# A graph layer's set-up: destination places in 128 rows, and the order of transfers on SP

## The chip, the cores and the metric

The kernel runs on one core of a Trainium2 chip. The metric is the time on the device in microseconds (us), as a median of runs. A core has engines with instruction queues of their own: PE (TensorE, matmuls), DVE (VectorE), ACT (ScalarE), POOL (GpSimd) and SP (SyncE). Each takes its queue in order. SP and ACT issue plain DMA transfers; POOL issues indirect ones (gathers by a list of row numbers). All share 16 DMA engines. An instruction can wait on semaphores that other engines or landed transfers raise, and what stands behind it in the same queue waits too.

## The reference

One message-passing layer of a graph network with 12,500 nodes, 412,500 edges (sorted by destination) and 96 channels:

```python
def _mlp(h, W, b, gamma, beta):
    h = relu(h @ W + b)
    mu, var = mean(h, axis=0), mean(square(h - mu), axis=0)
    return gamma * (h - mu) * rsqrt(var + EPS) + beta

node_feat = _mlp(x, W_node, ...)
edge_feat = _mlp(edge_attr, W_edge, ...)
message = concat([x[src], x[dst], edge_feat], axis=1)
message = _mlp(message, W_msg, ...)
agg = segment_sum(message, dst, 12500)
out = layernorm(x + agg + node_feat)
```

All normalisations are over the rows (all nodes or all edges), so statistics over every edge must be known before the edge features can be used in a message.

## The kernel before

Edges go in groups of 512 (four tiles of 128), four groups to a block: 806 groups, 202 blocks. The message's first product is split over the three parts of its input: a first table `p_tab` = x·W (source part) and a second table `q_tab` (destination part) are computed once per node and kept in DRAM. For each group, `p_tab`'s rows are gathered by source (L290, four indirect DMAs per group, on POOL). Destinations are sorted, so a group's edges fall into a window of 31 nodes; the window's rows of `q_tab` are loaded as they are, and an edge's place in its window picks its row through a matmul.

The places are needed in two forms. In one (`rel`) edges lie on partitions. In the other, `rel_d` in DRAM, they lie in a row, edge after edge, so that the main loop can load them beside the edges' attributes (L355). `rel_d` is computed by the loop at L194 to L201: the destinations `dlin` are loaded in two-group pieces of a layout with 101 rows of eight groups each (RW = 8·512), the groups' first nodes are loaded (`first`), DVE subtracts (L200), and ACT's queue stores (L201). The loads are on SP (L196, L198).

Before the main loop comes a set-up: 1. `table` for `p_tab`; 2. weights, `rel` and a check (`flag`); 3. the places; 4. `table` for `q_tab`, seven chunks of 14 column groups, each ending in a store on SP (L152); 5. `nodes`: matmuls of all nodes (L210), statistics (L212), normalisation (L218, L219), and 13 pieces `y0` = centred x + node feature, copied by DVE (L228) and stored on SP (L231); 6. `edge_norm`: the edge features' statistics, 202 steps in 26 chunks of eight. A chunk's attributes are loaded by SP (L246, two buffers), and a step is three matmuls (L250), one ACTIVATE (L253) and three BATCH_NORM_STATS2 (L255).

During all this POOL already gathers for the first 104 groups. They go, in 26 blocks of 16 gathers, into a tile `stage` with two buffers, and SP stores each block to DRAM (`spill`, L304); the main loop reads it back. After the 26 blocks POOL gathers 30 more groups into the ring that the main loop uses. Block k's gathers can start once store k-2 has landed.

The order of the instructions on SP and POOL is written out by hand in `fast` (the block under `manual_schedule`); the other engines' order comes from a scheduler. `blocks` is a generator: `next(store)` puts one block's gathers on POOL and its store on SP at that place in the program. As SP is in order, a store stands behind everything that SP issues before it, whatever that waits for.

The order is: places; second table with stores of blocks 0 and 1 behind its fourth and seventh chunk; stores 2 and 3; nodes with store 4 behind the sixth y0 and store 5 behind the thirteenth; edge statistics with one store ahead of the loads of chunks 2, 3, 4, 6, 7, 8, 9, 11 and so on (four of five); the last store; the ring.

The main loop works through all groups, per group four matmuls (L380), an addition of the gathered rows (L386), a relu (L387) and four matmuls that sum messages by place and collect the second moments (L395). The end normalises and adds y0.

Of the kernel before, what the change touches and what calls it, by code (L numbers as in the profile page):

```python
# [11 lines left out]
F32 = mybir.dt.float32  # L12
I32 = mybir.dt.int32
AF = mybir.ActivationFunctionType
OP = mybir.AluOpType
# [5 lines left out]
N, C, E, ED = 12500, 96, 412500, 4  # L21
EPS = 1e-5
P = 128
# [3 lines left out]
GT, GE, BG = 4, 512, 4  # L27
# [3 lines left out]
NTP, NGP = NBL * BG * GT, NBL * BG  # L31
EP = NGP * GE
EK = ED + 1
Q = 32
NS = 3
RW = 8 * GE

# [11 lines left out]
WN = 31  # L51
# [20 lines left out]
def gnn(ctx, tc, t):  # L72
    nc = tc.nc
    const = ctx.enter_context(tc.tile_pool(name="const", bufs=1))
    dram = ctx.enter_context(tc.tile_pool(name="dram", bufs=1, space=DRAM))
# [1 line left out]
    q_tab = dram.tile([NN, C], F32, name="q_tab")  # L77
    y0_d = dram.tile([-(-NB // NBY), P, NBY * C], F32, name="y0_d")
    spill = dram.tile([SPILL // BG, P, BG, GT * C], F32, name="spill")
    rel_d = dram.tile([1, EP], F32, name="rel_d")  # L80


    w_msg = const.tile([C, 3, C], F32, name="w_msg")
# [32 lines left out]
    base = const.tile([1, NGP], I32, name="base")  # L116
# [9 lines left out]
    def norm(aggr, gamma, beta, name):  # L126

        s = const.tile([C, 3], F32, name=f"norm_{name}")
        nc.scalar.activation(s[:, 2:3], aggr[:, 1:2], AF.Sqrt, bias=eps[:C], scale=1.0)  # L129
        nc.vector.reciprocal(s[:, 2:3], s[:, 2:3])  # L130
        nc.vector.tensor_mul(s[:, 0:1], s[:, 2:3], gamma)  # L131
        nc.vector.tensor_mul(s[:, 2:3], s[:, 0:1], aggr[:, 0:1])  # L132
        nc.vector.tensor_sub(s[:, 1:2], beta, s[:, 2:3])  # L133
        return s[:, 0:1], s[:, 1:2]


    def table(out, w, work, ps, queues):

        rows = out.rearrange("(p b) f -> p b f", b=NB)
        for c in range(0, NB, CH):  # L140
            r = work.tile([P, CH, C], F32, name="trow", bufs=3)
            for j, i in enumerate(range(0, CH, NBK)):
                n = min(NBK, CH - i)
                pt = ps.tile([P, NBK, C], F32, name="pt", bufs=4)
                for g in range(n):
                    k = COL[c + i + g]
                    nc.tensor.matmul(pt[:, g, :], xp[:, k:k + P], w, start=True, stop=True)  # L147
                if j % 2:
                    nc.scalar.activation(r[:, i:i + n, :], pt[:, :n, :], AF.Copy)  # L149
                else:  # L150
                    nc.vector.tensor_copy(r[:, i:i + n, :], pt[:, :n, :])
            queues[c // CH % len(queues)].dma_start(rows[:, c:c + CH, :], r)  # L152
            yield
# [9 lines left out]
    for i in range(NS):  # L163
        k, n = Q * i, C - Q * i
# [24 lines left out]
        nc.vector.tensor_reduce(most, po, axis=AX.X, op=OP.max)  # L189
        nc.vector.tensor_scalar(flag, most, 0.0, None, op0=OP.is_gt)  # L190

    with tc.tile_pool(name="lin", bufs=2) as work:
        shape = "o (p g e) -> (o p) g e"
        for i in range(0, RW // GE, 2):  # L194
            lin = work.tile([EP // RW, 2, GE], I32, name="lin")
            nc.sync.dma_start(lin, t["dlin"].rearrange(shape, g=RW // GE, e=GE)[:, i:i + 2, :])  # L196
            first = work.tile([EP // RW, 2], I32, name="first")
            nc.sync.dma_start(first, t["base"].rearrange("o (p g) -> (o p) g", g=RW // GE)[:, i:i + 2])  # L198
            rlin = work.tile([EP // RW, 2, GE], F32, name="rlin")
            nc.vector.tensor_tensor(rlin, lin, first.unsqueeze(2).to_broadcast([EP // RW, 2, GE]), op=OP.subtract)  # L200
            nc.scalar.dma_start(rel_d.rearrange(shape, g=RW // GE, e=GE)[:, i:i + 2, :], rlin)  # L201

    def nodes():

# [30 lines left out]
    def edge_norm():  # L235

        with tc.tile_pool(name="es", bufs=2) as work, tc.tile_pool(name="es1", bufs=1) as one, \
                tc.tile_pool(name="es_ps", bufs=2, space=PSUM) as ps:
            stats = one.tile([P, NS, NBL, 6], F32, name="estats")
            for b in range(NBL):  # L240
                if b % J == 0:
                    yield
                    ea = work.tile([P, J, GE], F32, name="ea")
                    n = min(J, NBL - b)
                    for i in range(NS):
                        nc.sync.dma_start(ea[Q * i:Q * i + 2 * EK, :n, :],  # L246
                                          t["ea"][EK * i:EK * (i + 2), b:b + n, :])
                pr = ps.tile([P, NS, GE], F32, name="pr")
                for i in range(NS):
                    nc.tensor.matmul(pr[:, i, :], wide[Q * i:Q * i + 2 * EK, :],  # L250
                                     ea[Q * i:Q * i + 2 * EK, b % J, :], start=True, stop=True)
                r = work.tile([P, NS, GE], F32, name="r")
                nc.scalar.activation(r, pr, AF.Relu)  # L253
                for i in range(NS):
                    nc.vector.bn_stats(stats[:, i, b, :], r[:, i, :])  # L255

            part = one.tile([P, NS, 2], F32, name="part")
            square = one.tile([P, NS], F32, name="square")
            for i in range(NS):
                nc.vector.bn_aggr(part[:, i, :], stats[:, i, :, :].rearrange("p a b -> p (a b)"))  # L260
            nc.vector.tensor_mul(square, part[:, :, 0], part[:, :, 0])
            nc.vector.tensor_add(part[:, :, 1], part[:, :, 1], square)
            pick = one.tile([P, NS, C], F32, name="pick")
            nc.vector.memset(pick, 0.0)
            for i in range(NS):
                for o in range(-P * i % C - C, P, C):
                    lo, hi = max(o, 0), min(o + C, P)
                    if lo < hi:
                        to = pick[:, i, lo - o:hi - o]
                        nc.vector.tensor_add(to, to, ident[:, lo:hi])  # L270
            pm = ps.tile([C, 2], F32, name="pr")
            for i in range(NS):
                nc.tensor.matmul(pm, pick[:, i, :], part[:, i, :], start=i == 0, stop=i == NS - 1)
            aggr = one.tile([C, 2], F32, name="eaggr")
            nc.vector.tensor_scalar(aggr, pm, float(NBL * GE) / E, None, op0=OP.mult)
            sq = one.tile([C, 1], F32, name="sq")
            nc.vector.tensor_mul(sq, aggr[:, 0:1], aggr[:, 0:1])
            nc.vector.tensor_sub(sq, aggr[:, 1:2], sq)
            nc.vector.tensor_scalar(aggr[:, 1:2], sq, 0.0, None, op0=OP.max)
            a_e, c_e = norm(aggr, v["g_edge"], v["beta_edge"], "edge")  # L280
            pb = ps.tile([1, C], F32, name="pr")
            nc.tensor.matmul(pb, c_e, w_msg[:, 2, :], start=True, stop=True)
            nc.vector.tensor_add(bias, pb, b_msg)
            nc.vector.tensor_scalar(w_e, w_msg[:, 2, :], a_e, None, op0=OP.mult)

    def fast(ring):
# [8 lines left out]
        def ahead_of(g):  # L295
            return gather(g, ring.tile([P, GT, C], F32, name="pg"))

        def blocks():

            for b in range(SPILL // BG):  # L300
                pg = ring.tile([P, BG, GT, C], F32, name="stage", bufs=2)
                for i in range(BG):
                    gather(b * BG + i, pg[:, i, :, :])
                nc.sync.dma_start(spill[b], pg.rearrange("p g a c -> p g (a c)"))  # L304
                yield


        store = blocks()
        with tc.manual_schedule(engines={ET.SP, ET.Pool}):
            with tc.tile_pool(name="tab_w", bufs=1) as work, tc.tile_pool(name="tab_ps", bufs=2, space=PSUM) as ps:  # L310
                for i, _ in enumerate(table(q_tab, w_msg[:, 1, :], work, ps, (nc.sync,))):
                    if i in (3, 6):
                        next(store)
            next(store)
            next(store)
            for i, _ in enumerate(nodes()):
                if i in (5, 12):
                    next(store)
            xpool.close()
            for i, _ in enumerate(edge_norm()):  # L320
                if i > 1 and i % 5:
                    next(store, None)
            for _ in store:
                pass
            got = {g: ahead_of(g) for g in range(SPILL, SPILL + RING)}

        with tc.tile_pool(name="fix", bufs=1) as fix, tc.tile_pool(name="msg", bufs=2) as work, \
# [92 lines left out]
            last, n, ahead = None, 0, SPILL + RING  # L420
# [20 lines left out]
            d = fix.tile([C, C], F32, name="d")  # L441
# [9 lines left out]
    def general():  # L451

        with tc.tile_pool(name="gd", bufs=1, space=DRAM) as gd, tc.tile_pool(name="gfix", bufs=1) as fix, \
# [136 lines left out]
            for b in range(NB):  # L590
# [7 lines left out]
                nc.vector.tensor_copy(agg[:, b * P:(b + 1) * P], px)  # L598

    fast(ring)  # L600
    rpool.close()
    bad = nc.values_load(flag, min_val=0, max_val=1, skip_runtime_bounds_check_because="a comparison's result")
# [4 lines left out]
    with tc.tile_pool(name="fin", bufs=2) as work, tc.tile_pool(name="fin_ps", bufs=2, space=PSUM) as ps:  # L607
# [6 lines left out]
        d = const.tile([C + 1, C], F32, name="dm")  # L614
# [3 lines left out]
        for i in range(0, NB, NBY):  # L618
            n = min(NBY, NB - i)
# [55 lines left out]
```

## Time and profile before

| | us |
|---|---|
| median of 11 runs | 5677.29 (5660.83 to 5681.44) |
| the profiled execution, its own time | 5676.63 |
| its span in the profile | 5674.9 |
| first gather / last of the 26 blocks' gathers | 54.6 / 1010.8 |
| first gather of the ring / of the main loop | 1012.1 / 1250.5 |
| busy: PE, DVE, ACT, POOL | 3489.2, 1838.8, 1128.7, 3067.8 |
| mean granted TensorE clock | 0.659 |

In the profile, a line of a group gives source line, engine, operation, tiles out<-in and count, then busy time and mean ns of one, then the idle time of the engine just before and what ended most of it. A line of the timeline gives start, duration, engine ("q" for its queue, where DMAs are issued), source line, operation, tiles and count, and in brackets the idle time before it and what ended it. "remote" there is an event whose sender the profile could not match. A line of the table by stretches gives the stretch, its length, the busy time of each engine, the granted clock of TensorE, the share of the DMA engines and the rate.

### The profile page before, as it was taken

The numbers are of one execution on the slowest core, as the hardware profiler recorded it, in microseconds if no ns is written. First come the engines' busy times: TensorE is split into PE (matmuls) and PEld (weight loads), VectorE is DVE, ScalarE is ACT, GpSimd is POOL, SyncE is SP. The second block draws the span as 40 slices with busy tenths as digits, with TensorE's granted clock in tenths as the row PEclk, the third lists the DMA queues.
The fourth block names the chain that finished last, engine by engine and source line by source line (L and its number), as shares of the span: only waits on it lengthen the run. The fifth ranks groups of instructions, "written<-read, shape, count | busy, mean of one in ns | idle before, by whom it ended". The sixth has DMA issues, their size and how long they took to land. (4 is left out here: it accounts for less than half of the span.)

```text
span 5674.9 us, 52840 instructions
## 1 busy us (share of the span) xinstructions
PE 3489.2 (61%) x16561; PEld 2604.3 (46%) x16561; DVE 1838.8 (32%) x4227; ACT 1128.7 (20%) x1304; POOL 3067.8 (54%) x3231
## 2 busy tenths in 40 slices
PE   3445565236766666676666666666666666666668
PEld 3331111015554555555445554545555455554547
DVE  1134555143232232322222322323233232322326
ACT  0123444121111111111111111111111111111113
POOL 2244444725655655555565556655655655556650
PEclk9955555556666666666676766666666676666767
DMA  3132232211111111111111111111111111111112
GB/s 118 73 95 59 63 67 65 52 36 40 42 41 42 37 42 41 40 42 40 37 41 41 42 41 37 42 40 42 42 41 41 38 42 40 41 41 36 42 34 73
DMA packets 154490, 271.03 MB, mean 48 GB/s; under 512 B 83723, under 2 KB 84107, under 8 KB 153198
## 3 DMA queue, kind: packets, MB, share of 16 engines
q0 software_dynamic: 103136, 158.62, 11.6%
q1 hardware_dynamic: 47572, 96.59, 6.0%
q10 hardware_dynamic: 3496, 12.36, 0.7%
q8 instruction: 136, 2.23, 0.2%
q14 instruction: 150, 1.23, 0.1%
HBM read 225.97 MB, written 41.37 MB: 47 GB/s over the span
## 5 line engine op out<-in xcount | busy, mean ns | idle before, releaser
L290 POOL DMA_INDIRECT pg<-p_tab,src x2807 | 2667.7, 950 | 1847.9 <-issue 759.3
L380 PE MATMUL z<-rhs,left 128*128 128x96 f32 x6446 | 1316.1, 348 | 644.6 <-issue 337.9
L380 PEld LDWEIGHTS z<-rhs,left 128*128 128x128 f32 x6446 | 1169.6, 260 | 1088.5 <-issue 596.7
L395 PE MATMUL pa<-h 128*97 128x128 f32 x6446 | 1240.1, 355 | 690.4 <-ACT h L387 495.3
L395 PEld LDWEIGHTS pa<-h 128*97 128x97 f32 x6446 | 1080.1, 228 | 750.1 <-ACT h L387 539.4
L387 ACT ACTIVATE h<-hs 128x384 f32<-128x384 f32 x806 | 419.8, 521 | 2980.8 <-DVE hs L386 1381.3
L398 DVE TENSOR_TENSOR agg<-pa,agg 97x31 f32 x806 | 151.2, 188 | 1948.6 <-remote 836.5
L290 POOL DMA_INDIRECT stage<-p_tab,src x416 | 399.1, 959 | 611.0 <-DMA spill<-stage 432.6
L386 DVE TENSOR_TENSOR hs<-z,pg 128x384 f32<-128x384 f32 x702 | 390.3, 556 | 999.1 <-remote 512.3
L250 PE MATMUL pr<-ea,wide 10*128 10x512 f32 x1212 | 406.6, 1108 | 412.4 <-ACT r L253 292.7
L371 PE MATMUL pr<-ea,we 6*127 6x512 f32 x1404 | 517.3, 813 | 157.7 <-issue 83.9
L255 DVE BATCH_NORM_STATS2 estats<-r 128x6 f32<-128x512 f32 x606 | 372.1, 681 | 445.8 <-ACT r L253 315.5
L373 ACT ACTIVATE left<-pr 96x2048 f32<-96x2048 f32 x202 | 376.5, 1864 | 621.7 <-remote 309.6
L374 DVE TENSOR_SCALAR left<-pr 31x2048 f32<-31x2048 f32 x202 | 462.9, 2292 | 45.1 <-ACT left L373 40.1
L250 PEld LDWEIGHTS pr<-ea,wide 10*128 10x128 f32 x1212 | 113.9, 307 | 703.7 <-ACT r L253 516.3
L253 ACT ACTIVATE r<-pr 128x1536 f32<-128x1536 f32 x202 | 292.7, 1451 | 589.9 <-remote 401.0
L371 PEld LDWEIGHTS pr<-ea,we 6*127 6x127 f32 x1404 | 131.6, 230 | 218.8 <-issue 128.1
L382 DVE TENSOR_TENSOR h<-rel,iota 128x124 f32<-128x124 f32 x806 | 208.1, 279 | 2.0 <-issue 0.4
L399 DVE TENSOR_TENSOR gram<-pa,gram 97x97 f32<-97x97 f32 x806 | 202.1, 251 | 12.9 <-DVE agg L398 6.5
L147 PE MATMUL pt<-w_msg,xp 96*128 96x96 f32 x392 | 85.5, 423 | 138.3 <-ACT trow L149 130.6
L147 PEld LDWEIGHTS pt<-w_msg,xp 96*128 96x128 f32 x392 | 84.1, 332 | 139.5 <-ACT trow L149 131.5
L371 PE MATMUL pr<-eae,we 6*127 6x512 f32 x208 | 75.9, 796 | 7.2 <-issue 7.0
(97 smaller groups left out, 507.2 us busy)
## 6 DMA issues: line engine op xcount, KB each, us to landing
pg<-p_tab,src POOLq DMA_INDIRECT x2807
spill<-stage SPq DMA_DIRECT2D x26, 768.0 KB
pb<-spill SPq DMA_DIRECT2D x26, 768.0 KB
rhs<-q_tab SPq DMA_DIRECT2D x806, 11.6 KB
ea<-in_ea SPq DMA_DIRECT2D x75, 160.0 KB
ea<-in_ea SPq DMA_DIRECT2D x352, 20.0 KB
stage<-p_tab,src POOLq DMA_INDIRECT x416
q_tab<-trow SPq DMA_DIRECT2D x7, 672.0 KB
```

The lines of the kernel that those rows point to most:

```text
L250: nc.tensor.matmul(pr[:, i, :], wide[Q * i:Q * i + 2 * EK, :], ea[Q * i:Q * i + 2 * EK, b % J, :], start=True, stop=True)
L253: nc.scalar.activation(r, pr, AF.Relu)
L255: nc.vector.bn_stats(stats[:, i, b, :], r[:, i, :])
L290: nc.gpsimd.indirect_dma_start(out=pg[:, i, :], out_offset=None, in_=p_tab[:, :], in_offset=bass.IndirectOffsetOnAxis(ap=src[:, k:k + 1], ...
L371: nc.tensor.matmul(pr[:, i, :], we[Q * i:Q * i + EK + 1, :], ea[Q * i:Q * i + EK + 1, :], start=True, stop=True)
L373: nc.scalar.activation(x[:C, :n, :], pr[:C, :n, :], AF.Relu)
L374: nc.vector.tensor_scalar(x[C:C + WN, :n, :], pr[C:, :n, :], 0.0, None, op0=OP.is_equal)
L380: nc.tensor.matmul(z[:, i, :], left[s % 2][:KR, g % BG, i * P:(i + 1) * P], rhs[:KR, s % 2, g % BG, :], start=True, stop=True)
L382: nc.vector.tensor_tensor(h[:, :, C + 1:C + 1 + WN], rel[:, g, :].unsqueeze(2).to_broadcast([P, GT, WN]), iota[:, None, :].to_broadcast([P ...
L386: nc.vector.tensor_add(hs[:, :n, :], z[:, :n, :], pg[:, :n, :])
L387: nc.scalar.activation(h[:, :n, :C], hs[:, :n, :], AF.Relu)
L395: nc.tensor.matmul(pa[:, :C + 1 + WN], h[:r, i, :C + 1], h[:r, i, :C + 1 + WN], start=i == 0, stop=i == n - 1)
```

## The change

1. The places are computed in 128 rows of seven groups (RW = 7; the destinations are padded on the host from 808 to 896 groups). `first` comes as an input of its own in that layout and is loaded once. Pieces have two groups each, the last one.
2. They stand in a function `places`, called after the second table and store 2. A piece's store is issued one piece later, on SP instead of ACT.
3. The stores of the blocks move: stores 0, 1, 2 behind the table's second, fifth and seventh chunk; store 3 behind the places; 4 and 5 behind the third and ninth y0; store 6 ahead of the loads of statistics chunk 0, and from then about 73 in a hundred chunks (three of four) have one ahead of them.

The number of gathers, stores and statistics steps is the same, and the main loop and the end are untouched.

```diff
-RW = 8 * GE
+RW = 7
...
-    rel_d = dram.tile([1, EP], F32, name="rel_d")
+    rel_d = dram.tile([1, P * RW * GE], F32, name="rel_d")
...
-    with tc.tile_pool(name="lin", bufs=2) as work:
-        shape = "o (p g e) -> (o p) g e"
-        for i in range(0, RW // GE, 2):
-            lin = work.tile([EP // RW, 2, GE], I32, name="lin")
-            nc.sync.dma_start(lin, t["dlin"].rearrange(shape, g=RW // GE, e=GE)[:, i:i + 2, :])
-            first = work.tile([EP // RW, 2], I32, name="first")
-            nc.sync.dma_start(first, t["base"].rearrange("o (p g) -> (o p) g", g=RW // GE)[:, i:i + 2])
-            rlin = work.tile([EP // RW, 2, GE], F32, name="rlin")
-            nc.vector.tensor_tensor(rlin, lin, first.unsqueeze(2).to_broadcast([EP // RW, 2, GE]), op=OP.subtract)
-            nc.scalar.dma_start(rel_d.rearrange(shape, g=RW // GE, e=GE)[:, i:i + 2, :], rlin)
+    def places():
+
+        with tc.tile_pool(name="lin", bufs=2) as work, tc.tile_pool(name="lin1", bufs=1) as one:
+            first = one.tile([P, RW], I32, name="first")
+            nc.sync.dma_start(first, t["first"])
+            rows = rel_d.rearrange("o (p g e) -> (o p) g e", g=RW, e=GE)
+            parts = [slice(i, min(i + 2, RW)) for i in range(0, RW, 2)]
+            lins = []
+            for i in range(len(parts) + 1):
+                if i < len(parts):
+                    n = parts[i].stop - parts[i].start
+                    lins.append(work.tile([P, n, GE], I32, name="lin"))
+                    nc.sync.dma_start(lins[i], t["dlin"][:, parts[i], :])
+                    rlin = work.tile([P, n, GE], F32, name="rlin")
+                    nc.vector.tensor_tensor(rlin, lins[i], first[:, parts[i]].unsqueeze(2).to_broadcast([P, n, GE]),
+                                            op=OP.subtract)
+                    lins[i] = rlin
+                if i:
+                    nc.sync.dma_start(rows[:, parts[i - 1], :], lins[i - 1])
...
-                    if i in (3, 6):
+                    if i in (1, 4, 6):
                         next(store)
-            next(store)
+            places()
             next(store)
             for i, _ in enumerate(nodes()):
-                if i in (5, 12):
+                if i in (2, 8):
                     next(store)
             xpool.close()
+            n = 0
             for i, _ in enumerate(edge_norm()):
-                if i > 1 and i % 5:
+                if 73 * i >= 100 * n:
                     next(store, None)
+                    n += 1
             for _ in store:
                 pass
```

More of the change, by code (lines that the diff above doesn't have):

```diff
@@ L652 @@
     give("dst", d.reshape(NTP, P).T)
-    give("base", np.minimum(d[::GE], N - WN).reshape(1, NGP))
-    give("dlin", d.reshape(1, EP))
+    base = np.minimum(d[::GE], N - WN)
+    give("base", base.reshape(1, NGP))
+    give("first", np.pad(base, (0, P * RW - NGP)).reshape(P, RW))
+    give("dlin", np.pad(d, (0, P * RW * GE - EP)).reshape(P, RW, GE))
     x = np.pad(np.asarray(inputs["x"]), ((0, NN - N), (0, 0))).reshape(P, NB, C).transpose(2, 1, 0)
```

## The prediction

> **What bounds the kernel now.** The chain that ended last, on the page, covers the final 60 us only (33 pieces from 5615.84 us, output matmuls of L624), so it says nothing of the start, where the change lies. I read the groups first, for what the gathers waited for:
>
> ```profile
> L290 POOL DMA_INDIRECT stage<-p_tab,src x416 | 399.1, 959 | 611.0 <-DMA spill<-stage 432.6
> ```
>
> POOL gathers 416 times into the spilled blocks, and stood idle 432.6 us until a store of a block had landed. Next the timeline around the longest of these pauses:
>
> ```profile
> 95.89 0.47 ACTq L201 DMA_DIRECT2D rel_d<-rlin  x1
> 96.76 26.84 SPq L196 DMA_DIRECT2D lin<-in_dlin  x1
> ...
> 130.05 15.27 SPq L196 DMA_DIRECT2D lin<-in_dlin  x1
> 145.37 15.53 SPq L198 DMA_DIRECT2D first<-in_base  x1
> ...
> 211.68 18.55 SPq L152 DMA_DIRECT2D q_tab<-trow  x4
> ...
> 230.53 0.33 SPq L304 DMA_DIRECT2D spill<-stage  x1
> ...
> 235.50 0.95 POOL L290 DMA_INDIRECT stage<-p_tab,src  x1 [137.62 <-DMA spill<-stage]
> ```
>
> Block 0 of the gathers was full at about 75 us, but its store is issued on SP at 230.53, behind the loads of the places (`lin`, `first`) and four stores of the second table, which in turn waited for `rel_d<-rlin`. With two `stage` buffers POOL could fill two blocks and then stood for 137.62 us. The table by stretches shows that nobody else used that time (columns: stretch, its length, busy us of PE, PEld, DVE, ACT, POOL, granted clock, DMA share, GB/s):
>
> ```profile
> 98.00:211.00 113.00, 0.00 (x0) 0.00 (x0) 4.08 (x4) 0.27 (x1) 0.00 (x0) 1.00 0.06 25
> 211.00:235.50 24.50, 24.23 (x114) 24.23 (x114) 5.08 (x10) 3.40 (x9) 0.00 (x0) 1.00 0.35 145
> ```
>
> For 113 us the DMA share is 0.06 of 16 engines at 25 GB/s: one engine's work. The transfers of 101 rows ran one after another, 404 KB in about 15.5 us each. Last, the rest of the start, from two rows of ACT's timeline in the edge statistics, inside a run of gathers and outside one:
>
> ```profile
> 1049.14 1.45 ACT L253 ACTIVATE r<-pr 128x1536 f32<-128x1536 f32 x1 [15.35 <-remote]
> 1065.94 1.45 ACT L253 ACTIVATE r<-pr 128x1536 f32<-128x1536 f32 x1 [15.35 <-remote]
> ```
> ```profile
> 717.38 1.45 ACT L253 ACTIVATE r<-pr 128x1536 f32<-128x1536 f32 x1 [0.31 <-PE pr L250]
> 719.32 1.45 ACT L253 ACTIVATE r<-pr 128x1536 f32<-128x1536 f32 x1 [0.48 <-PE pr L250]
> ```
>
> From 1012 to 1162 us, while 120 gathers run without a gap, one step of the statistics (three matmuls, one ACTIVATE, three BATCH_NORM_STATS2) takes 16.8 us, because PE's release comes late; at 717 us, POOL idle, it takes 1.85 us. In each run of gathers PE keeps its pace for about 7.5 us (five steps by 8.0 us of the run at 480.6, the next at 13.0), then drops to a tenth. So in the start gathers and PE work nearly exclude each other, and its length is a sum:
>
> 54.6 (first table) + 672.3 (536 gathers, at 1.25 us plus a few long ones) + 434.5 (POOL's pauses) = 1161.4 us, then 88.7 us (last 14 statistics steps, aggregation, first loads) to the main loop's first gather at 1250.5. The pauses are 196.2 us before the edge statistics have begun (137.6, 9.7, 34.7, 12.1, 2.1) and 238.3 in nine pieces within them. The main loop takes the other 4424 us; nothing in it changes. What counts is how much of pauses and tail goes.
>
> **The change, part by part.**
>
> *Places removed from their old position.* Eight loads on SP and four stores on ACT leave the stretch from 74 to 211 us. The second table's matmuls, whose row buffers waited for these transfers, can start at 74.4 us (PE issued the first 14 there already) instead of being evacuated from 210.6.
>
> *Places put behind the second table's last store, on SP.* One load of `first`, four of `lin`, four stores: nine issues of 0.35 us. They have 128 rows, and 128-row transfers of this trace are fast: the table's 672 KB moved at about 440 GB/s in the DMA view. So 512 KB need 1.2 us plus landing. Issue to next use was 5.0 us for a stage store (230.53 to 235.50); I take 4 us for each. A store waits for the DVE subtract of its part, the third part for the first part's store (two buffers): 4 + 1.2 + 4 + 1.2 + 4 + 1.2 + 4 = 20 us on SP from first issue to last; bounds 10 (all overlapped) and about 160 (at the old 26 GB/s, eight times 20 us). Queued behind on SP are store 3 and through it block 5's gathers; block 4 gathers for 20 us meanwhile and is the cover. At twice the price block 5 starts 20 us late.
>
> *The four subtracts* take 1.23 us each as before (L200). One gather beside such a subtract took 1.95 us instead of 0.95 (94.69 us). Three of the four fell into the long pause; now all lie beside gathers: +3 us, between 0 and 4.
>
> *Stores 0 to 6 placed anew.* Walking through with 6.2 us per table chunk (18.55 us between the first and fourth store), 20 us per block, 5 us from store to gather, and PE at full pace for 7.5 us of each run of gathers and at a fifth after that (in such a run one node matmul came per 4.9 us against 0.86):
> - table chunks 0 and 1 end near 99, store 0 lands at 105; POOL, full at 97.9, pauses 7.
> - chunks 2 to 4 end at 128, store 1 lands at 133, block 2 ended at 125: pause 8.
> - chunks 5 and 6 end at 141, store 2 lands at 146, before block 3 ends at 153: no pause. Places from 141 to 163, store 3 lands at 168, block 4 ends at 173: no pause.
> - Node matmuls run against blocks 3 to 5: about 10 of 25 by 193, the rest by 206. Norm and update take 18.4 us (305.2 to 323.6), two copies and the memset of agg (10.5) follow, then the third copy and store 4 at 239, landing 244: pause 51, where the old kernel had 34.7. This is the largest new wait: block 6 needs store 4, and that stands behind the third y0.
> - Store 5, behind nine blocks of y0, costs 10; store 6 nothing.
>
> Sum 76 instead of 196.2: -120 us. The statistics would start at 282 instead of 388.
>
> *Stores 7 to 25, three in four chunks instead of four in five.* A cycle of old was 137 us: two runs of 40 us with 7 statistics steps in each, and two pauses of 57 us together for the other 26 (48 us at 1.85, and 4.6 us of landing per pause). A cycle is now one run of two blocks and one of one (6 steps, as in the run at 480.6). Per three blocks 13 steps lie in runs, against 10.5. Over six cycles 15 steps more ride along: -28 us. It costs some 2.5 landing waits of 4.6 us: +12. Together -16; bounds -30 and +10 (the tail's alignment).
>
> Sum: -120 - 16 + 3 = -133 us. Here a rule speaks differently. The Trainium skill, page "SBUF — State Buffer", section "Who interferes with whom", has only VectorE and GpSimd contend and says that PE and ACT never wait on anyone. By it PE would work through the runs of gathers at 1.85 us a step: no second-order pattern gain, pause 51 down to about 20, and -148 us. The rows (16.8 us against 1.85) contradict it for this stage, whatever the mechanism; I take the rows.
>
> Against the profiled execution's own 5676.6 us (span 5674.9) this gives 5543.6. The runs' median is 0.7 us above it: 5544 us.
>
> **Rivals.**
>
> *Pauses come back (gain 60 to 110, about 5590).* Each front pause depends on where PE loses its pace. If PE is held from the first gather on instead of after 7.5 us, each store is late by some 8 us more over five stores. For it: y0's copies took 4 to 13 us late in a run (366 to 383 us) against 3.4. Against it: ten steps at full pace in the run at 396.3.
>
> *More goes (gain 160 to 185, about 5505).* The pause of 51 shrinks if the node matmuls get further ahead of blocks 4 and 5, since at 141 us the granted clock may still be 1.00, as it was until about 280.
>
> *The change doesn't do what it says (about 5675).* If transfers of 128 rows also ran at 26 GB/s, the places would hold SP for 160 us in their new position, block 5 would wait 137 and nothing was won. Against it: 440 GB/s for the 128-row stores of the same queue.
>
> *Slower, by the main loop's clock.* Its granted clock is 0.65 to 0.68 in all stretches, and PE is 65% busy. Should the loop, entered 130 us earlier and after less rest, get 0.64 instead of 0.66, 4424 us times 0.02/0.64 are +138 and eat the gain: that is the point from which it decides. At 0.63 the time is 5677 - 133 + 211 = 5755. Against it: stretches from 2000 to 5000 us show 0.67 three times, long after any rest.
>
> **How the numbers follow.** Likeliest -133: 0.66. Pauses come back: 0.15. More goes: 0.11. No effect: 0.03. Slower: 0.05. A measurement of this kernel tells about 0.2% (11 us) from no change. Faster: 0.66 + 0.15 + 0.11 = 0.92; within: 0.03; slower: 0.05. The likeliest case spans 5518 to 5568 (places' 10 us either way, pattern +26 or -14, pause 51 by 10). The range adds most of both neighbours, 5505 to 5590, and leaves out the 8 in 100 of the last two and about a tenth at the two ends.
>
> **What the new profile would show.** Right: no pause on POOL over 60 us; the statistics' first ACTIVATE near 295 (282 plus the 13 from loads to first step before) instead of 401.7; the main loop's first gather near 1118; places' transfers together under 25 us at far over 26 GB/s; a pause of about 50 before block 6; main loop as long as before within 10 us. Wrong: pauses over 20 us among the table's stores, a store 3 issued later than 180 us, or a main loop longer by more than 20 us at a lower clock.

## The result

The changed kernel takes 5545.73 us (median of 8 runs, 5544.19 to 5550.3) against 5674.93 of the kernel before (31 runs): ratio 0.9775, 95% interval 0.9765 to 0.9785, so 129 us less. The forecast was 5544. The profiled execution took 5547.81 us with a span of 5546.1 (before: 5676.63 and 5674.9), 128.8 us less.

First the groups of the profile after: the gathers into spilled blocks, which had waited 432.6 us for stores.

```profile
L299 POOL DMA_INDIRECT stage<-p_tab,src x416 | 395.4, 951 | 494.7 <-DMA spill<-stage 311.2
```

121.4 us of that wait are gone. Next SP's timeline, from the table to the stores of y0:

```profile
86.19 16.20 SPq L152 DMA_DIRECT2D q_tab<-trow  x2
102.69 0.33 SPq L313 DMA_DIRECT2D spill<-stage  x1
...
140.72 0.33 SPq L313 DMA_DIRECT2D spill<-stage  x1
141.10 0.94 SPq L196 DMA_DIRECT2D first<-in_first  x1
143.15 0.96 SPq L204 DMA_DIRECT2D lin<-in_dlin  x2
...
157.11 2.18 SPq L210 DMA_DIRECT2D rel_d<-rlin  x2
162.63 1.39 SPq L313 DMA_DIRECT2D spill<-stage  x1
225.52 15.07 SPq L240 DMA_DIRECT2D y_d<-y0s  x3
240.89 0.32 SPq L313 DMA_DIRECT2D spill<-stage  x1
```

Store 0 is issued at 102.69 instead of 230.53. The places' nine transfers are issued between 141.10 and 159.3, 18 us, and store 3 goes out at 162.63. The table by stretches shows at what rate (columns as before; in the first row are also the store of a block and the gathers):

```profile
141.00:163.00 22.00, 16.05 (x30) 5.15 (x28) 6.02 (x7) 7.51 (x11) 16.72 (x18) 0.90 0.86 299
163.00:211.00 48.00, 18.89 (x20) 4.11 (x20) 16.01 (x28) 10.55 (x16) 25.47 (x27) 0.50 0.12 32
892.00:1041.00 149.00, 18.75 (x54) 4.58 (x54) 16.92 (x27) 13.05 (x9) 112.70 (x120) 0.50 0.18 46
```

In the place of 25 GB/s and a DMA share of 0.06 stand 299 GB/s and 0.86. The second row holds 20 records of node matmuls, which are ten products (the profile has two records for each), in 48 us; gathers fill the first 33.6 us of it, with six of the ten. The third row is the ring's run of gathers without a gap, in which PE is busy 18.75 of 149 us. POOL's timeline shows the pauses that are left:

```profile
107.66 0.94 POOL L299 DMA_INDIRECT stage<-p_tab,src  x1 [10.41 <-DMA spill<-stage]
...
136.46 0.94 POOL L299 DMA_INDIRECT stage<-p_tab,src  x1 [9.13 <-DMA spill<-stage]
...
245.27 0.94 POOL L299 DMA_INDIRECT stage<-p_tab,src  x1 [48.67 <-DMA spill<-stage]
...
274.02 0.94 POOL L299 DMA_INDIRECT stage<-p_tab,src  x1 [9.09 <-DMA spill<-stage]
```

The pause of 137.62 us is gone. The longest is now the one ahead of block 6, 48.67, which waits for the store behind the third y0. ACT's timeline in the statistics, the first step, two inside the last run of gathers, two after it:

```profile
293.50 1.45 ACT L262 ACTIVATE r<-pr 128x1536 f32<-128x1536 f32 x1 [67.50 <-PE pr L259]
...
1014.70 1.45 ACT L262 ACTIVATE r<-pr 128x1536 f32<-128x1536 f32 x1 [14.65 <-remote]
1031.50 1.45 ACT L262 ACTIVATE r<-pr 128x1536 f32<-128x1536 f32 x1 [15.35 <-remote]
...
1068.52 1.45 ACT L262 ACTIVATE r<-pr 128x1536 f32<-128x1536 f32 x1 [0.31 <-PE pr L259]
1070.45 1.45 ACT L262 ACTIVATE r<-pr 128x1536 f32<-128x1536 f32 x1 [0.48 <-PE pr L259]
```

A step in the run still takes 16.8 us, one after it 1.9. The statistics start 108 us earlier (293.50 against 401.7).

### The profile page after: what moved, and what is told of

Read it like the earlier page. It is cut to its first block, busy times and chain, and to the rows that moved or that the text cites. A ratio compares the mean times of both kernels' runs of the same rounds, so it can differ in the third digit from the quotient of the medians.

```text
span 5546.1 us, 52832 instructions
## 1 busy us (share of the span) xinstructions
PE 3507.6 (63%) x16561; PEld 2608.2 (47%) x16561; DVE 1836.4 (33%) x4227; ACT 1127.4 (20%) x1304; POOL 3057.5 (55%) x3231
```

## The set-up as a sum, before and after

| us | before | predicted change | after | measured change |
|---|---|---|---|---|
| first gather | 54.6 | 0 | 55.2 | +0.6 |
| 536 gathers | 672.7 | +3 | 668.1 | -4.6 |
| pauses ahead of the statistics | 196.2 | -120 | 84.3 | -111.9 |
| pauses within the statistics | 238.3 | with the tail -16 | 233.9 | -4.4 |
| tail to the main loop's first gather | 88.7 | | 74.7 | -14.0 |
| sum: main loop's first gather | 1250.5 | -133 | 1116.2 | -134.3 |
| main loop and end | 4424.4 | 0 | 4429.9 | +5.5 |

The pauses are gaps between one gather's end and the next one's start where they exceed 1.45 us; "after" is their sum in POOL's timeline. The 672.3 us of the prediction were 0.4 short: the last of the 536 gathers ends at 1161.85 us, not at 1161.4.

## The experiments

The theory to be tested has two parts. (a) What gained the time is the shape of the places' transfers (128 rows instead of 101), which took the long pause away; their position and the stores' order alone gain little. (b) The rest of the set-up's length is set by PE and the gathers nearly excluding each other. Rivals: the order of stores gained it; or PE's slow steps come from something else that a break in the gathers doesn't lift.

The first four kernels, and the last four, ran on chips on which the kernel before takes 4309.49 and 4304.06 us, the middle four on one where it takes 5673.69, like the chip of the result; so each is compared with the kernel before on its own chip, and expectations in microseconds that were reckoned from 5675 can't hold for the first four. The changed kernel itself, without an alteration, ran only where the kernel before takes about 5674 us.

**Each part of the change alone.** The stores in their old order, all else as changed:

```diff
-                    if i in (1, 4, 6):
+                    if i in (3, 6):
...
             places()
             next(store)
+            next(store)
...
-                if i in (2, 8):
+                if i in (5, 12):
...
-                if 73 * i >= 100 * n:
+                if i > 1 and i % 5:
```

> The changed kernel with the stores of blocks in the old order (behind the fourth and seventh chunk of the table, two behind the places, behind the sixth and thirteenth y0, four of five statistics chunks). Theory (gathers and PE work exclude each other, so pauses of POOL add up): store 0 comes two table chunks later, pause 22 us instead of 10; store 5 behind the thirteenth y0 costs some 15 more; the old pattern in the statistics costs the 18 us of edge pauses and tail back. About 30 us slower than the changed kernel: 5575 us (5560 to 5590). Rival, the stores' order is immaterial: 5546. Rival, the stores' order brought most of the gain: 5630 or more.

Measured: 4188.92 us against 4309.49, ratio 0.9721 (0.9704 to 0.9737). Pauses ahead of the statistics: 8.4, 9.3, 2.8, 2.1 us.

The kernel before with the new order of stores, the same lines turned round:

> The kernel before with only the stores moved; places stay at their old position in 101 rows. Theory: the pause of 137 us shrinks only by the two table chunks that store 0 no longer waits for (12 us), and the new pattern gives its 18 us: 5645 us (5625 to 5660). Rival, the stores' order brought most of the gain: 5590 or less. Rival, it is worth nothing alone: 5675.

Measured: 4300.81 us, ratio 0.9981 (0.9971 to 0.9991). POOL's first pause is still 126.8 us.

The changed kernel, with the places in 101 rows of eight groups at their new position:

```diff
-RW = 7
+RW = 8
+PR = 101
...
-                    lins.append(work.tile([P, n, GE], I32, name="lin"))
+                    lins.append(work.tile([PR, n, GE], I32, name="lin"))
```

(and PR for P in `first`, `rlin`, `rel_d` and the padding.)

> The changed kernel with the places in 101 rows of eight groups at the new position. Theory: each transfer runs on one DMA engine at 26 GB/s, 15.5 us; store 3 waits on SP for six of them, some 95 us instead of 22, and the node statistics for all eight (buffers in the same memory), so norm comes some 75 us later, of which a part is used by PE: 5605 us (5580 to 5625). Rival, the row count is immaterial and only the position counted: 5546.

Measured: 4296.05 us, ratio 0.9967 (0.9954 to 0.9979). SP's timeline of this kernel, with the places behind the table:

```profile
143.76 17.86 SPq L205 DMA_DIRECT2D lin<-in_dlin  x1
161.66 15.97 SPq L211 DMA_DIRECT2D rel_d<-rlin  x1
177.67 15.96 SPq L205 DMA_DIRECT2D lin<-in_dlin  x1
194.15 30.24 SPq L211 DMA_DIRECT2D rel_d<-rlin  x2
224.68 15.69 SPq L314 DMA_DIRECT2D spill<-stage  x1
```

and POOL's:

```profile
256.50 0.94 POOL L300 DMA_INDIRECT stage<-p_tab,src  x1 [98.56 <-DMA spill<-stage]
```

Each transfer keeps SP for some 16 us, the store of block 3 waits behind them until 224.68, and POOL pauses 98.56 us and then 28.4 more. The pause of the old kernel has only moved from in front of block 2 to in front of block 5. Between 160 and 190 us the DMA share is 0.06 at 26 GB/s: 404 KB in 16 us, the work of one engine of 16.

The kernel before, with 128 rows of seven groups at the old position (loads ahead of the second table, stores on ACT; `n` is the number of groups in a piece, two and in the last piece one; other lines of the loop are adapted alike and left out):

```diff
-RW = 8 * GE
+RW = 7
...
-            nc.sync.dma_start(lin, t["dlin"].rearrange(shape, g=RW // GE, e=GE)[:, i:i + 2, :])
+            nc.sync.dma_start(lin, t["dlin"][:, i:i + n, :])
```

> The kernel before with only the layout changed: 128 rows of seven groups, at the old position ahead of the second table, stores on ACT, block stores in the old order. Theory: the transfers take some 25 us instead of 136, the table starts near 100 us, store 0 lands near 130: pause about 33 us instead of 137.6, the rest as before: 5570 us (5555 to 5590). Rival, only the position counts: 5675.

Measured: 4190.89 us, ratio 0.9725 (0.9709 to 0.9742). The first pause is 17.0 us.

What follows, for this chip: the number of rows alone gives 118.6 us (4309.49 to 4190.89), the same within the intervals as rows and position together (120.6). The order of stores alone gives 8.7, position and order without the rows 13.4. On a chip like the result's the four weren't run, so there the split between rows, position and order stays argued from the trace.

**The same chip or another.** These four brought up a question that I hadn't asked: why the same kernel takes 1365 us less there. The table by stretches of the first experiment, in its statistics:

```profile
240.00:600.00 360.00, 360.00 (x1117) 101.81 (x1114) 340.52 (x560) 270.07 (x187) 271.74 (x288) 0.50 0.52 111
```

POOL gathers without a pause (288 gathers in 360 us, 1.25 us each), and beside them PE is busy 360 of 360 us and finishes 187 steps, 1.93 us each, at the same granted clock of 0.50. On the result's chip PE did 18.75 us in 149 beside such gathers. So part (b) of my theory held on some of these chips and not on others. Each chip was met in one session, so whether it is the chip or a condition that it was in is not shown either. The main loop differs as well: 3427 us there (4181.3 less 754.4) against 4424 to 4430.

Next, on a chip of the result's kind, the changed kernel once more, as the base of three others:

> The changed kernel itself, on the chip of these runs, to have all its parts beside each other. Where the kernel before takes about 5675 us (gathers hold PE back): 5546 us, ratio 0.9775. Where it takes about 4309 us (gathers and PE run side by side, POOL's unbroken gathers set the time): only POOL's pauses count; the pause of 127 us goes and one of some 20 us ahead of store 4 comes: 4190 us (4175 to 4200), ratio 0.972.

Measured: 5549.47 us against 5673.69, ratio 0.978 (0.9763 to 0.9796). Pauses of 10.8, 9.1, 49.3, 9.0 us, the first statistics step at 294.4, the main loop's first gather at 1124.3.

**Rests between the gathers.** If gathers in an unbroken run hold PE back, short breaks should free it. In the set-up POOL sets an unused tile of 128x512 (`rest`) twice behind every four gathers:

```diff
                     in_offset=bass.IndirectOffsetOnAxis(ap=src[:, k:k + 1], axis=0))
+            if g < SPILL + RING:
+                nc.gpsimd.memset(rest, 0.0)
+                nc.gpsimd.memset(rest, 0.0)
             return pg
```

> The changed kernel with two GpSimd memsets of a spare 128x512 tile (about 1 us together) behind every four gathers of the set-up, 134 times. Where gathers hold PE back, theory (PE loses its pace only in an unbroken run of gathers): statistics steps keep 1.85 us, the set-up ends some 100 to 170 us earlier, 5380 to 5450 us. Rival (gathers hold PE whatever their spacing): the rests only stretch the gathers, 5546 to 5690 us. Where POOL's gathers set the time (before about 4309): 134 rests come on top, about 4190 plus 120 to 150 us, both theories alike.

Measured: 5274.84 us in one execution. POOL's timeline of this kernel:

```profile
500.21 0.94 POOL L300 DMA_INDIRECT stage<-p_tab,src  x1 [0.30 <-issue]
501.16 0.54 POOL L304 MEMSET rest<- 128x512 f32 x1
501.75 0.52 POOL L305 MEMSET rest<- 128x512 f32 x1
502.43 0.95 POOL L300 DMA_INDIRECT stage<-p_tab,src  x1 [0.16 <-issue]
```

and ACT's at the same place:

```profile
503.88 1.45 ACT L263 ACTIVATE r<-pr 128x1536 f32<-128x1536 f32 x1 [0.54 <-PE pr L260]
505.59 1.45 ACT L263 ACTIVATE r<-pr 128x1536 f32<-128x1536 f32 x1 [0.26 <-PE pr L260]
507.57 1.45 ACT L263 ACTIVATE r<-pr 128x1536 f32<-128x1536 f32 x1 [0.54 <-ACT r L263]
```

A break of 1.2 us after 5 us of gathers, and steps beside gathers take 1.85 us instead of 16.8. The statistics end at 692.5 us, before the gathers do; no pause over 3.5 us is left; the main loop's first gather comes at 886.0 instead of 1124.3. The 134 rests cost about 140 us of POOL's time and still save 238 in the set-up. That is more than the 100 to 170 expected. The main loop, which has no rests here, is 37 us shorter as well (4387 against 4425), which is not explained.

The same rests behind every four gathers of the whole kernel (the `if` left out):

> As the rests in the set-up, but behind every four gathers of the whole kernel (806 times). Where gathers hold PE back, theory: runs of 12 and 16 gathers in the main loop no longer stop PE, and the loop gets shorter by several hundred us, below 5200. Rival: no change of the loop or longer, 5546 to 5800. Where POOL's gathers set the time: 806 rests on top, about 4190 plus 700 to 850 us.

Measured: 5236.23 us in one execution, 39 less than with rests in the set-up alone; several hundred were expected, and that missed. The main loop takes 4348 us, far from the other chip's 3427: its order of POOL's instructions is set by the scheduler, which moves settings of the tile together, and what else keeps PE waiting there was not found.

**Is a pause a loss?** In the changed kernel, the pause of 49 us ahead of block 6 looks like the next gain. Three stores ahead of the nodes (3, 4, 5) instead of one take it away:

```diff
             places()
             next(store)
+            next(store)
+            next(store)
...
-                if i in (2, 8):
+                if i in (5, 11):
...
-                if 73 * i >= 100 * n:
+                if i and 73 * i >= 100 * n:
```

> The changed kernel with stores 3, 4 and 5 all behind the places (blocks 6 and 7 can then be gathered while norm and update run, which need no PE), stores 6 and 7 behind the sixth and twelfth y0. Where gathers hold PE back: the pause of 49 us ahead of block 6 goes, the node matmuls end 12 us later: 5515 to 5535 us. Where POOL's gathers set the time: the pause of some 20 us ahead of block 6 goes: 15 to 25 us under the changed kernel.

Measured: 5561.84 us, ratio to before 0.9801 (0.9785 to 0.9817): 12 us slower than the changed kernel, not faster. SP's timeline:

```profile
159.56 39.92 SPq L313 DMA_DIRECT2D spill<-stage  x3
249.53 23.26 SPq L240 DMA_DIRECT2D y_d<-y0s  x6
273.10 0.32 SPq L313 DMA_DIRECT2D spill<-stage  x1
```

and the last step of the statistics on ACT:

```profile
1090.92 1.45 ACT L262 ACTIVATE r<-pr 128x1536 f32<-128x1536 f32 x1 [0.20 <-PE pr L259]
```

POOL gathered five blocks without a break from 135.9 to 239.5, which was the aim, and its last gather into the 26 blocks began 49 us earlier (849.9 against 898.9). A pause of 37.9 us came ahead of block 8 instead. But the nodes' matmuls were held meanwhile: the first statistics step came 21 us later (315.7), and when the ring's last gather began at 999.7, 38 steps were still to do. The tail grew from 74.7 to 136.2 us. Pauses ahead of the statistics fell by 14, those within them by 38, the tail took 62. On this chip the time of a pause that PE was using came back elsewhere. (The edit also moves the stores within the statistics forward; a pattern of stores fitted to the new start was not tried.)

**The change without the hold.** The kernel before, with the rests of the sixth experiment:

> The kernel before, with the rests of the sixth experiment: POOL sets an unused tile twice (about 1 us) behind every four gathers of the set-up. Theory: the change's gain is the transfers of 101 rows taken out of POOL's first pause, and it stands whether or not PE is held back: this kernel keeps a first pause of about 130 us, loses all its other pauses over 10 us, and enters the main loop about 120 us later than the changed kernel with rests (886.0 us), near 1005; it takes about 5395 us. Rival: the gain belongs to the changed order of the stores under a held PE; then with PE free both kernels with rests come out within 40 us of each other, 5275 to 5315. (Where the kernel before takes about 4310 us, PE isn't held and each rest only costs: about 4430 us.)

Measured, on a chip of the 4304 us kind: 4445.3 us, ratio 1.0331 (1.031 to 1.0351). The 134 rests cost 141 us, 1.05 each, where PE isn't held. POOL's timeline:

```profile
236.01 0.95 POOL L291 DMA_INDIRECT stage<-p_tab,src  x1 [130.43 <-issue]
```

The long pause is there, 131.6 us between gathers (130.43 behind the rest), and no other is over 5 us. The main loop's first gather comes at 1015.6. The changed kernel with the same rests in its set-up, in the last experiment below, has it at 886.0: with PE free in both, the change is worth 129.6 us in the set-up. The rival, a gain under 40 us, is out where PE is free; that it also holds for a chip like the result's rests on the changed kernel's set-up with rests being as long there (886.0).

A rest per eight gathers (`and g % 2` added), and one setting instead of two:

> The changed kernel with the same two settings of a spare tile, but behind every eight gathers instead of four: 67 us less of rests. PE keeps its pace for some 7.5 us of a run of gathers, and eight gathers take 10 us. Theory (a rest of 1 us gives back a fixed 7.5 us at full pace): statistics at 4 steps full pace and 3 us held per 11 us, about 2.4 us a step against 2.0; they end before the gathers do, POOL alone bounds the set-up, and the main loop's first gather comes about 67 us sooner than with a rest per four gathers (886.0), near 820 to 840; 5210 to 5230 us. Rival (one rest gives back only about two or three steps, as the queue of what is held has to drain): about 4 us a step, statistics 800 us long and not hidden; set-up 1000 us or more, 5390 us or more. (Where the kernel before takes about 4310 us: about 4255.)

Measured: 4241.01 us, ratio 0.9856 (0.9836 to 0.9876).

> The changed kernel with one setting of the spare tile (0.54 us) behind every four gathers instead of two. If what counts is that POOL does something else than issue gathers, half the length serves as well: POOL's set-up is shorter by 134 times 0.5 us or so, main loop's first gather near 820, 5210 us. If what counts is how long the gathers rest, PE is partly held again: statistics steps of 3 us or more in the runs of gathers, set-up between 890 and 1100, 5280 to 5500 us. (Where the kernel before takes about 4310 us: about 4255.)

Measured: 4224.43 us, ratio 0.9817 (0.9798 to 0.9837). Both ran where PE isn't held, so they tell the price of rests (the fewer or shorter, the nearer to the 4189 of the first experiment) and nothing on how long a rest must be. That stays open.

Rests in the whole kernel, timed:

> The changed kernel with two settings of the spare tile behind every four gathers in the set-up and in the main loop, timed. It took 5236.23 us in one look, 39 us less than with rests in the set-up alone. Theory (in the main loop, too, PE is held in part by runs of gathers): the median stays between 5220 and 5250, ratio near 0.923. Rival: the 39 us were this one execution's; 5265 to 5285, ratio 0.93. (Where the kernel before takes about 4310 us: 4189 plus 800 rests of 1 us, about 4990.)

Measured: 4990.21 us, ratio 1.1595 (1.1576 to 1.1615), as reckoned for such a chip: 806 rests cost 801 us against 4189 (again the first experiment's, with the old order of stores). Its set-up ends at 886.0 us, exactly where the sixth experiment's did on the other chip (886.0). With rests the two chips' set-ups are equal; without them they were 1124 and, with the old order of stores, 754. So rests in the whole kernel are no version to hand on: 438 us faster than the kernel before on one chip (one execution), 686 slower on another. The change is faster on the first kind by 124 to 129 us. On the other kind its variant with the old order of stores is faster by 121, and even with the rests of the two experiments before this one it is faster than the kernel before by 63 and 80.

## Why the prediction was right

**What goes is time in which nobody works.** The step from the stretch at 98 to 211 us, one DMA engine busy and all else idle, to "the pause goes" held: -111.9 us for the front against -120. The experiments on the other kind of chip show that there it is the rows: 101 rows in the new position keep a pause of 98.56, 128 rows in the old one have 17.0. The Trainium skill (page "DMA: Bandwidth & Descriptors", section "Why a DMA increments its semaphore by 16 and not by 1") gives a reason that fits: a transfer is split over the largest number of engines up to 16 that divides the slowest dimension of both its sides, so 101 rows, a prime, get one engine and 128 rows get 16. The rates (25 and 26 GB/s against 299 in the stretch of the places) agree.

**The places on SP**: 20 us reckoned from 141, 18 measured from 141.10. **The front's order of stores**: landings reckoned at 105, 133, 146, 168, 244 us; POOL went on at 107.66 and 136.46, store 2 was issued at 140.72, store 3 at 162.63, and POOL went on again at 245.27. The pauses of 7, 8, 51 and 10 were 10.4, 9.1, 48.7 and 9.1. Short waits of 2.1, 1.5 and 3.4 us among the gathers when the statistics begin were not in the sum; with the 4.5 us that the first two pauses were longer, less the 3 us that the other two were shorter, they make up the 8 us between -120 and -111.9.

**The node matmuls under block 3 to 5** were not as reckoned, though their end was. PE was to keep its pace for 7.5 us of the run of gathers, with about 10 of 25 products begun by 193 us and the rest done by 206. The run begins at 136.46, and PE kept its pace until 153.9: 21 products were begun by 193. (The 7.5 us came from the statistics; in the old kernel's run from 265.0 the node matmuls had kept theirs until about 280.) But the last four ended at 207.5, since PE stayed slow for some us after the gathers had stopped at 196.6. That the pause came to 48.7 against 51 is therefore in part luck.

**The subtracts beside gathers** were the step with the wrong sign: +3 reckoned, -4.6 measured in the 536 gathers. Only one gather beside the four subtracts was slow, by 0.5 us (1.47). And ten gathers of 1.12 to 1.38 us, near 310 us in the old kernel, have no counterpart, which is 2 us. They lay beside the ten updates of the node features on DVE (L218, 307.8 to 322.2); in the changed kernel these fall into POOL's pause (210.2 to 224.6), and in the eighth experiment, where POOL gathers through them, ten gathers of 1.12 to 1.39 us are back. The estimate rested on a single slow gather and left this term out.

**Pattern and tail**: -16 reckoned, -18.4 measured, but the larger part in the tail (14.0), not in the cycles. The right sum of two parts whose sizes I couldn't tell apart, so here too the agreement is partly luck. The same goes for the whole: the front gained 8 us less than reckoned, the gathers 7.6 and pattern and tail 2.4 more, and so -133 met -134.3.

**The rule against the rows.** The rule of the Trainium skill (page "SBUF — State Buffer", section "Who interferes with whom"), "PE and ACT never wait on anyone", would have given -148, as the prediction reads it. The rows' -133 was nearer to the -128.8 measured, and the hold of PE stands in the trace after (16.8 us a step). Yet on the other chips the rule describes what is seen (1.93 us a step beside gathers), and there the gain was 119 to 121 (rows alone, and rows with position), without the rule's 15 us more: no hold was there for the change to lighten, and in the second experiment, with the places at their old position, no pause but the first is over 5.4 us, where the old kernel had 35 and 12. The section is on the ports of the on-chip memory; whether the hold has to do with them no run here shows.

**The main loop** was 5.5 us longer, inside the 10 given. The granted clock in the stretches from 2000 to 5000 us is 0.68, 0.66, 0.68 against 0.67 three times: the slower rival by the clock doesn't show. Nor does the rival that more goes: node matmuls did run at clock 1.00, from 145 to 155 us, but were held afterwards at ten in 48 us, and the pause stayed 49.

One sentence of mine was too simple: that what counts is how much of pauses and tail goes. As a sum it is true. As a guide to the next change it failed in the eighth experiment, in which pauses shrank by 52 us and the tail grew by 62.

## What to carry to other kernels

Before a stretch of slow transfers is hidden or reordered, look at its DMA share: 0.06 of 16 engines is one engine, and a row count that 16 divides (here 101 rows of eight groups padded to 128 of seven) removed more than the order of queues did. Ask of each pause what other engines do in it: a pause in which all are idle is a gain when it goes, one in which another engine catches up comes back elsewhere. And time a schedule on more than one chip if it depends on how two engines share something: rests in the whole kernel gained 6% over the changed kernel on one chip and lost 19% on another (there against the variant with the old order of stores).

## What the runs showed that I had not expected

- The same kernel takes 5674 to 5675 us on one kind of chip and 4304 to 4309 on two other chips. The difference shows where gathers run without a gap: PE does a statistics step in 16.8 us on the one and in 1.93 on the other, with a granted clock of 0.50 in both. On the slow one ACT waits for an event that comes long after the matmul's modelled end, so either the matmul or its signal is late; the trace doesn't tell which. The cause was not found.
- Two settings of an unused tile, 1.2 us with their gaps, behind every four gathers lift the hold in the set-up wholly (886.0 us on both chips).
- The 1.00 that the clock column shows early on is not a granted clock. In the changed kernel the trace has no record of the clock before 145 us (before 263 us in the kernel before), and such a stretch is printed as 1.00. The node matmuls tell the difference:

```profile
140.00:145.00 5.00, 4.88 (x6) 1.81 (x7) 0.00 (x0) 1.43 (x3) 3.77 (x4) 1.00 0.88 317
145.00:150.00 5.00, 5.00 (x13) 1.89 (x12) 1.07 (x1) 3.74 (x6) 3.77 (x4) 1.00 0.78 267
```

PE is busy in both rows, with 6 records in the first and 13 in the second. So the 1.00 over the idle stretch from 98 to 211 us of the kernel before says nothing, and "1.00 until about 280" in the prediction was 263 to 284. The recorded 1.00 falls to 0.50 when the dense matmuls thin out (about 284 us before, 158 after, 143 in the first experiment) and does not return during the statistics, though PE is busy 360 of 360 us from 240 to 600 in that experiment. As 0.50 stands both where PE is held and where it isn't, the clock does not explain the hold.
